# A selective scan: some input terms from a selected diagonal of B on TensorE, the skip term on TensorE, and one product with C for each pair of states

## The chip, the cores and the metric

The kernel runs on one core of a Trainium2 chip. The time is device time in microseconds (us) of one execution. Five engines work beside each other and meet only at semaphores: TensorE (PE in the profile; PEld is its weight load), VectorE (DVE), ScalarE (ACT), GpSimd (POOL) and SyncE (SP), which here issues all the DMAs. Each engine takes its instructions in program order.

## The reference

The whole program has four layers over an input of 4 images of 64 x 64 pixels with 96 channels: two convolution layers with a selective scan in four directions, and two layers of attention and feed-forward on tokens. The change lies in the selective scans of the first two layers. Cut to what matters, with K = 4 directions, 192 inner channels d and 16 states n:

```python
def _selective_scan(u, delta, A, Bs, Cs, Dp):
    ...
    def step(h, inp):
        u_l, dl, b_l, c_l = inp
        dA = jnp.exp(dl[..., None] * A)
        h = dA * h + (dl * u_l)[..., None] * b_l[:, :, None, :]
        y = jnp.einsum('bkdn,bkn->bkd', h, c_l)
        return (h, y)
    _, ys = lax.scan(step, h0, (u_t, d_t, B_t, C_t))
    ys = jnp.moveaxis(ys, 0, 3)
    return ys + Dp[None, :, :, None] * u
...
xs = jnp.concatenate([xs2, jnp.flip(xs2, axis=-1)], axis=1)
x_dbl = jnp.einsum('bkdl,kcd->bkcl', xs, x_proj_weight)
dts, Bmat, Cmat = jnp.split(x_dbl, [DT_RANK, DT_RANK + D_STATE], axis=2)
dts = jnp.einsum('bkrl,kdr->bkdl', dts, dt_projs_weight)
delta = jax.nn.softplus(dts + dt_projs_bias[None, :, :, None])
A = -jnp.exp(A_logs).reshape(K, D_INNER, D_STATE)
ys = _selective_scan(xs, delta, A, Bmat, Cmat, Dp)
```

So for each of 16 states, each channel holds a running value h over 4096 points: h = exp(delta A) h + (delta u) B. The output is the sum over the states of h C, plus the skip term D u.

## The kernel before, in words

Two images are worked on together (a pair), so there are four scans: two layers by two pairs. `PairScan.scan` does one. Its 192 channels by two images are laid out in three tiles of 128 partitions: tile j = 0 is image 0's first 128 channels, j = 1 is image 1's, and j = 2 holds the last 64 channels of both. A scan walks 4 directions k, in each 4 chunks ci of T = 1024 points, in each the three tiles j: 48 steps, named by `at`. Steps with j = 0 or 1 are called own here, those with j = 2 shared. A step has 16 states in 8 groups of NG = 2, named by `g`, with first state n0.

For each state a group needs three things of 128 x 1024. `da` is exp(delta A), made by ScalarE (`exp_of`, L522). `bp`, in PSUM, is delta u B; `cb` is C, read back by DMA from `crow` in DRAM and spread over the partitions. Who makes delta u B is written out by a letter for each state (L45, read by `maker`):

- V: TensorE spreads B over the partitions into bp by a product with the 0/1 table `sel` (two products of 512 columns); VectorE multiplies bp by `du` (L712).
- A: ScalarE makes the product with time on the partitions, where B is one scalar for a partition, in eight pieces `x` from `dut`, the transposed du (`outer`, L541); TensorE transposes the pieces back into bp.
- G: a DMA spreads B into `bb`, GpSimd multiplies it by du into `dbu` (`start_dbu`, L570), and bp then takes exp(delta A) instead.

VectorE runs the recurrence as one `tensor_tensor_scan` of 1024 points for each state (L715). GpSimd copies the last point to `last` for the next chunk (L728; not in the last chunk of a direction), then multiplies h by cb, one instruction for each state (L730). TensorE adds h up over the 16 states by transposing it into the PSUM tile `yp` (`add_up`, L603), with a lag of LAG = 3 groups; in direction 0 yp begins with the skip term, which ScalarE makes (`start_skip`, L631), and later with the sum of the directions before (`kept`). ScalarE copies yp out to `ysum` (`finish_sum`, L661). The projections for the next chunk and delta, du, dut of the next step are cut into pieces that are driven at fixed places between the groups (`project`, `discretise`, `drive`).

The program order is written out by hand. In group g's turn (loop at L680) come: the two bp of g; the sums of group g - 3; then, for g + 1, x and da (ScalarE), the loading of cb, and dbu (GpSimd); VectorE's products and the two scans of g; driven pieces; GpSimd's copy and products of g. What limits how far an engine runs ahead: bp has 2 buffers, da 4, x 2, h 4, cb 3, yp 1, dbu and bb 1. The wrapper `InOrder` (L56 to L73) keeps this order, and it is why all these instructions bear line L71 in the profile.

Of the kernel before, what the change touches and what calls it, by code (L numbers as in the profile page):

```python
# [16 lines left out]
F32 = mybir.dt.float32  # L17
BF16 = mybir.dt.bfloat16
# [8 lines left out]
HW = 64  # L27
# [14 lines left out]
LAG = 3  # L42


OWN, SHARED = "VAVAVAAGVAVAVAVA", "VGVAVAVGVAVGVAVV"  # L45
NT = L // 128
HID = 4 * C
EPS = 1e-5
# [36 lines left out]
class ScanLayer:  # L85


    def __init__(self, tc, pw, dram, x_src, w, n):
# [12 lines left out]

        self.amat = pw.tile([128, 2, K * NS], F32, name=f"amat{n}")
        nc.scalar.activation(self.amat, par[:, :, P_A : P_A + K * NS], AF.Exp)
        nc.vector.tensor_scalar(self.amat, self.amat, -1.0, None, ALU.mult)
        self.dsum = pw.tile([128, 2, 1], F32, name=f"dsum{n}")
        nc.vector.tensor_reduce(self.dsum, par[:, :, P_D : P_D + K], mybir.AxisListType.X, ALU.add)


class GroupNorm:
# [260 lines left out]
class PairScan:  # L370
# [5 lines left out]
    def __init__(self, tc, pk, pq, pd, cst, ident, u, layer, pr):  # L376
        self.tc, self.pk, self.pq, self.pd = tc, pk, pq, pd
        self.cst, self.ident, self.u = cst, ident, u
        self.par, self.amat, self.dsum = layer.par, layer.amat, layer.dsum
# [106 lines left out]

    def scan(self, stage, nc):
        tc, ident, steps, projected, made = self.tc, self.ident, self.steps, self.projected, self.made
        amat, dsum, w, y, weights, chunk_of = self.amat, self.dsum, self.w, self.y, self.weights, self.chunk_of
# [26 lines left out]
        of = (0, 128, 64)  # L516

        def maker(g, i):
            at, n0 = groups[g]
            return (SHARED if steps[at][2] == 2 else OWN)[n0 + i]  # L520
# [37 lines left out]
            return cb  # L558

        bbs = {}  # L560

        def start_bb(g):

            at, n0 = groups[g]
            for i in range(NG):
                if maker(g, i) == "G":
                    bbs[g, i] = p2.tile([128, 1, T], F32, name="bb", bufs=1)
                    spread(bbs[g, i], projected[at // 3][2], steps[at][2], 2 * NS + n0 + i)

        def start_dbu(g):  # L570
            out = {}
            for i in range(NG):
                if (g, i) in bbs:
                    out[i] = p2.tile([128, T], F32, name="dbu", bufs=1)
                    nc.gpsimd.tensor_tensor(out[i], made[groups[g][0]][1], bbs.pop((g, i))[:, 0], ALU.mult)
            return out

        def start_bp(g, i, xs):


            at, n0 = groups[g]
            _, _, j = steps[at]
            bp = pm.tile([128, T], F32, name="bp", bufs=2)
            if maker(g, i) == "G":
                exp_of(bp, g, i)
            elif maker(g, i) == "A":
                for t in range(T // 128):
                    nc.tensor.transpose(bp[:, 128 * t : 128 * t + 128], xs[i][:, t], ident)
            else:
                for hf in range(2):  # L590
                    cols = slice(512 * hf, 512 * hf + 512)
                    nc.tensor.matmul(
                        bp[:, cols],
                        sel[:, n0 + i, of[j] : of[j] + 128],
                        projected[at // 3][1][:, cols],
                        start=True,
                        stop=True,
                    )
            return bp
# [3 lines left out]
        def add_up(g, i, h):  # L603

            at, n0 = groups[g]
            n = n0 + i
            if n == 0:
                sums[at] = yp = pm.tile([128, T // 128, 128], F32, name="yp")
                if at in skips:
                    onto_time(yp, skips.pop(at), True, False)  # L610
                else:
                    before = kept.pop(at)
                    for t in range(0, T // 128, 4):
                        nc.tensor.matmul(yp[:, t : t + 4], ident, before[:, t : t + 4], start=True, stop=False)
            onto_time(sums[at], h[:, i], False, n == NS - 1)

        def onto_time(yp, v, first, final):

            for t in range(T // 128):
                nc.tensor.matmul(  # L620
                    yp[:, t],
                    v[:, 128 * t : 128 * t + 128],
                    ident,
                    start=first and t % 4 == 0,
                    stop=final and t % 4 == 3,
                    is_transpose=True,
                )

        skips = {}

        def start_skip(at):  # L631

            k, _, j = steps[at]
            if k == 0:
                skips[at] = p2.tile([128, T], F32, name="skip", bufs=1)
                nc.scalar.mul(
                    skips[at].rearrange("p (a b) -> p a b", b=HW), projected[at // 3][0][j], dsum[:, j // 2]
                )

        def places(at, tile_):  # L640
# [25 lines left out]

        for g in range(2):
            start_bb(g)
        ahead, cb_next, dbu_next = start_ahead(0), start_cb(0), start_dbu(0)
        hs = {}  # L670

        def sum_of(g):
# [7 lines left out]
        for g, (at, n0) in enumerate(groups):  # L680
# [12 lines left out]
            (da, xs), cb, dbu = ahead, cb_next, dbu_next  # L693
            if g + 2 < len(groups):
                start_bb(g + 2)

            bps = [start_bp(g, i, xs) for i in range(NG)]
            if g >= LAG:
                sum_of(g - LAG)
            if n0 == 0:  # L700
                start_skip(at)
            if n0 == NS - NG:
                drive(discretising, n0)
                drive(projecting, (j, n0))
            if g + 1 < len(groups):
                ahead, cb_next, dbu_next = start_ahead(g + 1), start_cb(g + 1), start_dbu(g + 1)

            hs[g] = h = p2.tile([128, NG, T], F32, name="h", bufs=LAG + 1)
            du = made[at][1]
# [16 lines left out]
            drive(projecting, (j, n0))  # L726
            if not final:
                nc.gpsimd.tensor_copy(last[j][:, n0 : n0 + NG], h[:, :, 0] if rev else h[:, :, T - 1])  # L728
            for i in range(NG):
                nc.gpsimd.tensor_tensor(h[:, i], h[:, i], cb[:, i], ALU.mult)  # L730
        for g in range(len(groups) - LAG, len(groups)):
            sum_of(g)
        finish_sum(len(steps) - 1)
# [206 lines left out]
def hybrid_kernel(ctx: ExitStack, tc: tile.TileContext, a):  # L940
# [14 lines left out]
    with ExitStack() as scans:  # L955
        pw = scans.enter_context(tc.tile_pool(name="s_w", bufs=1))
        pn = scans.enter_context(tc.tile_pool(name="s_n", bufs=1))
        units = []
        for n in range(2):
            layer = ScanLayer(tc, pw, dram, x, {k: a[f"l{n}_{k}"] for k in ("par", "wi", "wx", "wdt", "wo")}, n)  # L960
            units += [(layer, pr) for pr in range(NB // 2)]
            x = layer.x_dst
        units[0][0].after = units[2][0]
        with ExitStack() as scanning:
            pk = scanning.enter_context(tc.tile_pool(name="s_k", bufs=2))
            pu = scanning.enter_context(tc.tile_pool(name="s_u", bufs=1))
            pq = scanning.enter_context(tc.tile_pool(name="s_q", bufs=1))
            pd = scanning.enter_context(tc.tile_pool(name="s_d", bufs=2, space=DRAM))
            cst["sel"] = pu.tile([NP, NS, 256], BF16, name="sel")
            nc.sync.dma_start(out=cst["sel"], in_=a["c_sel"])  # L970
            cst["ident16"] = pu.tile([128, 128], BF16, name="ident16")
            nc.vector.tensor_copy(cst["ident16"], ident)
            u = [pu.tile([128, L], F32, name=f"u{j}") for j in range(3)]
            before = None
            for unit in units:
                scan = PairScan(tc, pk, pq, pd, cst, ident, u, *unit)
                between_scans(tc, cst, ident, half, pn, u, before, scan, unit)
                scan.run()
                before = unit
        token_layers(tc, cst, ident, half, x, before, a)  # L980


def constants():
# [10 lines left out]
    group = np.where(at[:, None] // 3 == at[None] // 3, np.float32(1) / np.float32(3), np.float32(0))  # L994
    heads = np.where(at[:, None] // 16 == at[None] // 16, np.float32(0.25), np.float32(0))
    return {
        "c_sel": sel.reshape(NP, NS, 256),
        "c_group": group.astype(np.float32),
        "c_heads": heads.astype(np.float32),
    }  # L1000
# [93 lines left out]
```

## Time and profile before

| What | Value |
|---|---|
| Time, median of 3 runs | 10596.84 us (10596.55 to 10597.79) |
| Profiled execution, first to last instruction | 10592.1 us |
| Instructions | 142441 |
| Mean granted TensorE clock | 0.885 of full |
| HBM traffic | 199 GB/s over the span |

How to read the lines below: in a group, the shape after the names is the output's and then the input's, `x` gives the count, after the first bar stand the time in which the group was busy (us) and the mean length of one instruction (ns), and after the second bar the engine's idle time just before these instructions, with what ended it. In a view in order of time, the columns are start (us), length (us), engine, line, operation, tiles, shape and count, and in brackets idle time with what ended it. In the list of waits: who waited for whom, then us in total, how often, and the longest. In a view by windows: the stretch, its length, then for each engine busy us and count of instructions.

### The profile page before, as it was taken

The page shows a single profiled execution, that of the slowest core. Times are in us where ns is not written, and L with a number is a line of the kernel's source. Part 1 is how long each engine was busy: PE and PEld are TensorE (multiplying, and loading weights), DVE is VectorE, ACT ScalarE, POOL GpSimd, SP SyncE. Part 2 cuts the span into 40 slices and gives each one's busy share as a digit, 9 for nine tenths or more (in the row PEclk, how much of TensorE's full clock was granted, in tenths as well). Part 3 has the DMA queues.
Part 4 walks back from the last instruction along what each step waited for, and adds up shares of the span by engine and source line. Part 5 has one row for each costly group of instructions (what it writes and reads, how often), then busy time and mean ns, then how long its engine had stood idle before and what let it go on. Part 6 is the DMA issues. An engine that isn't in the chain of part 4 may idle for free. (4 is left out here: it accounts for less than half of the span.)

```text
span 10592.1 us, 142441 instructions
## 1 busy us (share of the span) xinstructions
PE 8027.2 (76%) x47648; PEld 5946.6 (56%) x47648; DVE 9610.8 (91%) x6922; ACT 8761.4 (83%) x18779; POOL 9023.9 (85%) x5298
## 2 busy tenths in 40 slices
PE   7777777777777777777877777777877777777666
PEld 4555555554555555555555555555555565555554
DVE  8999999998999999998899999999799999999755
ACT  6888888885988888887788888888688888888666
POOL 3999999993999999997599999999399999999645
PEclk9888898989888898998888988898888989899877
DMA  5677777776677777777567777777667777777710
GB/s 155 208 212 216 220 220 218 219 218 164 205 212 212 218 220 218 217 220 210 158 206 213 219 220 220 223 213 216 162 207 212 216 213 225 221 217 213 195 32 25
DMA packets 905174, 2120.41 MB, mean 200 GB/s; under 512 B 330582, under 2 KB 640152, under 8 KB 706712
## 3 DMA queue, kind: packets, MB, share of 16 engines
q1 hardware_dynamic: 904440, 2111.30, 69.5%
q8 instruction: 378, 6.19, 0.3%
q14 instruction: 356, 2.92, 0.1%
HBM read 1949.56 MB, written 161.48 MB: 199 GB/s over the span
## 5 line engine op out<-in xcount | busy, mean ns | idle before, releaser
L71 POOL TENSOR_TENSOR h<-h,cb 128x1024 f32<-128x1024 f32 x3072 | 7196.5, 2367 | 226.4 <-issue 62.6
L71 DVE TENSOR_TENSOR_SCAN h<-da,last,bp 128x1024 f32<-128x1024 f32 x2064 | 4736.6, 2335 | 146.7 <-PE bp L71 22.8
L71 ACT ACTIVATE x<-dut,bt 128x128 f32<-128x128 f32 x12288 | 3495.9, 371 | 1.4 <-PE bp L71 1.1
L71 PE MATMUL yp<-ident,h 128*128 128x128 f32 x24576 | 3359.4, 297 | 10.5 <-POOL h L71 10.5
L71 PEld LDWEIGHTS yp<-ident,h 128*128 128x128 f32 x24576 | 3188.5, 157 | 126.6 <-issue 76.6
L71 ACT ACTIVATE da<-delta,amat 128x1024 f32<-128x1024 f32 x2752 | 3062.3, 1139 | 96.6 <-DVE h L71 95.8
L71 PE MATMUL bp<-ident,x 128*128 128x128 f32 x10240 | 1678.5, 316 | 1294.1 <-DVE h L71 956.8
L71 PEld LDWEIGHTS bp<-ident,x 128*128 128x128 f32 x10240 | 1361.3, 163 | 1854.8 <-ACT x L71 1017.4
L71 DVE TENSOR_TENSOR bp<-du,bp 128x1024 f32<-128x1024 f32 x1472 | 1780.5, 1214 | 259.8 <-PE bp L71 257.8
L71 DVE TENSOR_TENSOR_SCAN h<-da,bp 128x1024 f32<-128x1024 f32 x688 | 1537.7, 2275 | 49.9 <-ACT da L71 9.6
L71 PE MATMUL bp<-bparts,sel 96*128 96x512 bf16 x2944 | 920.5, 398 | 756.3 <-DVE h L71 740.4
L71 PEld LDWEIGHTS <-sel 96*128 96x128 bf16 x2944 | 226.8, 100 | 1550.2 <-DVE h L71 1037.8
L71 ACT ACTIVATE bp<-delta,amat 128x1024 f32<-128x1024 f32 x320 | 358.1, 1119 | 526.3 <-DVE h L71 524.6
L71 POOL TENSOR_TENSOR dbu<-du,bb 128x1024 f32<-128x1024 f32 x320 | 755.7, 2362 | 0.0
L71 DVE TENSOR_TENSOR_SCAN h<-bp,last,dbu 128x1024 f32<-128x1024 f32 x240 | 558.9, 2329 | 16.9 <-POOL dbu L71 15.9
L71 PE MATMUL xps<-u,wx 128*76 128x512 f32 x720 | 532.2, 824 | 0.0
L71 POOL COPY last<-h 128x2 f32<-128x2 f32 x1152 | 217.7, 189 | 357.2 <-DVE h L71 355.5
L81 POOL TENSOR_TENSOR ln_rs<-ln_ve,half 128x4 f32<-128x4 f32 x64 | 89.8, 1403 | 483.1 <-DVE ln_ve L79 405.9
L71 ACT ACT_TABLE_LOAD x380 | 487.5, 1283 | 15.9 <-PE bp L71 9.2
L71 POOL TENSOR_TENSOR du<-delta,u 128x1024 f32<-128x1024 f32 x188 | 496.8, 2642 | 0.0
L71 PE MATMUL dps<-cdt,wdt 12*128 12x512 f32 x752 | 433.6, 656 | 0.0
L71 ACT COPY ysum<-yp 128x1024 f32<-128x1024 f32 x192 | 194.5, 1013 | 287.1 <-PE yp L71 287.1
(159 smaller groups left out, 6312.6 us busy)
## 6 DMA issues: line engine op xcount, KB each, us to landing
cb<-crow SPq DMA_DIRECT2D x1024, 1024.0 KB
cb<-crow SPq DMA_DIRECT2D x1024, 512.0 KB
bb<-crow SPq DMA_DIRECT2D x384, 256.0 KB
bb<-crow SPq DMA_DIRECT2D x128, 512.0 KB
y<-ysum SPq DMA_DIRECT2D x192, 256.0 KB
kept<-y SPq DMA_DIRECT2D x160, 256.0 KB
y<-ysum SPq DMA_DIRECT2D x64, 512.0 KB
zt<-zg SPq DMA_DIRECT2D x64, 384.0 KB
```

The costliest lines, as they stand in the source:

```text
L71: return self.tc.keep_in_program_order(getattr(self.engine, op)(*args, **kwargs))
L81: nc.gpsimd.tensor_tensor(rs, ve, half, ALU.pow)
```

## The change

Three things change. In own steps three states of 16 get a new letter D, in place of V or A, the G goes, and the A move, so that the pairs read VD AA VD AA VD AA VA VA instead of VA VA VA AG VA VA VA VA. For a D, GpSimd's `affine_select` builds from the column of B (`bt`, time on the partitions) eight diagonal matrices of 128 x 128, and TensorE multiplies `dut` by them into bp; nobody else touches that bp before the scan. The selects of group g + 1 stand on GpSimd behind dbu of g + 1 and ahead of the copy and product of g. Second, the skip term is added by TensorE as a product of u with a diagonal of D that is made once a layer; ScalarE's instruction goes. Third, the product with C is one GpSimd instruction of 128 x 2048 for a group. Besides, the table sel is half as wide, and for own steps one column of it is spread as the weight.

```diff
@@ -42,7 +42,7 @@
-OWN, SHARED = "VAVAVAAGVAVAVAVA", "VGVAVAVGVAVGVAVV"
+OWN, SHARED = "VDAAVDAAVDAAVAVA", "VGVAVAVGVAVGVAVV"
...
@@ -104,6 +104,9 @@
         nc.vector.tensor_reduce(self.dsum, par[:, :, P_D : P_D + K], mybir.AxisListType.X, ALU.add)
+        self.skip = pw.tile([128, 2, 128], F32, name=f"skip{n}")
+        for s in range(2):
+            nc.vector.tensor_scalar(self.skip[:, s], ident, self.dsum[:, s], None, ALU.mult)
...
@@ -558,6 +559,7 @@
+        zero = self.tc.nc.gpsimd.to_reg(0.0)
...
+        def start_diagonals(g):
+
+            at, n0 = groups[g]
+            j = steps[at][2]
+            out = {}
+            for i in range(NG):
+                if maker(g, i) == "D":
+                    out[i] = p2.tile([128, T // 128, 128], F32, name="dg", bufs=1)
+                    col = NS * j + n0 + i
+                    nc.gpsimd.affine_select(
+                        out=out[i],
+                        in_=projected[at // 3][4][:, :, col : col + 1].to_broadcast([128, T // 128, 128]),
+                        compare_op=ALU.is_equal,
+                        fill=zero,
+                        base=0,
+                        pattern=[[0, T // 128], [-1, 128]],
+                        channel_multiplier=1,
+                    )
+            return out
...
-        def start_bp(g, i, xs):
+        def start_bp(g, i, xs, dgs):
...
+            elif maker(g, i) == "D":
+                for t in range(T // 128):
+                    nc.tensor.matmul(
+                        bp[:, 128 * t : 128 * t + 128], made[at][2][:, t], dgs[i][:, t], start=True, stop=True
+                    )
             else:
+                if j == 2:
+                    chosen = sel[:, n0 + i]
+                else:
+                    chosen = sel[:, n0 + i, D1 * j : D1 * j + 1].to_broadcast([NP, 128])
...
-                        sel[:, n0 + i, of[j] : of[j] + 128],
+                        chosen,
...
                 sums[at] = yp = pm.tile([128, T // 128, 128], F32, name="yp")
-                if at in skips:
-                    onto_time(yp, skips.pop(at), True, False)
+                k, ci, j = steps[at]
+                if k == 0:
+                    for t in range(T // 128):
+                        there = T * ci + 128 * t
+                        nc.tensor.matmul(
+                            yp[:, t],
+                            self.u[j][:, there : there + 128],
+                            self.skip[:, j // 2],
+                            start=t % 4 == 0,
+                            stop=False,
+                        )
                 else:
...
-        def start_skip(at):
-
-            k, _, j = steps[at]
-            if k == 0:
-                skips[at] = p2.tile([128, T], F32, name="skip", bufs=1)
-                nc.scalar.mul(
-                    skips[at].rearrange("p (a b) -> p a b", b=HW), projected[at // 3][0][j], dsum[:, j // 2]
-                )
...
-            bps = [start_bp(g, i, xs) for i in range(NG)]
+            bps = [start_bp(g, i, xs, dgs) for i in range(NG)]
             if g >= LAG:
                 sum_of(g - LAG)
-            if n0 == 0:
-                start_skip(at)
...
                 ahead, cb_next, dbu_next = start_ahead(g + 1), start_cb(g + 1), start_dbu(g + 1)
+                dgs_next = start_diagonals(g + 1)
...
                 nc.gpsimd.tensor_copy(last[j][:, n0 : n0 + NG], h[:, :, 0] if rev else h[:, :, T - 1])
-            for i in range(NG):
-                nc.gpsimd.tensor_tensor(h[:, i], h[:, i], cb[:, i], ALU.mult)
+            nc.gpsimd.tensor_tensor(h, h, cb, ALU.mult)
...
-            cst["sel"] = pu.tile([NP, NS, 256], BF16, name="sel")
+            cst["sel"] = pu.tile([NP, NS, 128], BF16, name="sel")
...
-    sel = np.zeros((3, 2, NS, NS, 2, 128), ml_dtypes.bfloat16)
+    sel = np.zeros((3, 2, NS, NS, 2, D1), ml_dtypes.bfloat16)
```

More of the change, by code (lines that the diff above doesn't have):

```diff
@@ L85, with __init__ @@
 class ScanLayer:
-    def __init__(self, tc, pw, dram, x_src, w, n):
+    def __init__(self, tc, pw, dram, ident, x_src, w, n):
         nc = tc.nc
@@ L378, in __init__ @@
         self.cst, self.ident, self.u = cst, ident, u
-        self.par, self.amat, self.dsum = layer.par, layer.amat, layer.dsum
+        self.par, self.amat, self.skip = layer.par, layer.amat, layer.skip
         self.w, self.y = layer.w, layer.y[pr]
@@ L488, in scan @@
         tc, ident, steps, projected, made = self.tc, self.ident, self.steps, self.projected, self.made
-        amat, dsum, w, y, weights, chunk_of = self.amat, self.dsum, self.w, self.y, self.weights, self.chunk_of
+        amat, w, y, weights, chunk_of = self.amat, self.w, self.y, self.weights, self.chunk_of
         sel = self.cst["sel"]
@@ L515, in scan @@
         groups = [(at, n) for at in range(len(steps)) for n in range(0, NS, NG)]
-        of = (0, 128, 64)
         def maker(g, i):
@@ L614, in add_up, with onto_time @@
                         nc.tensor.matmul(yp[:, t : t + 4], ident, before[:, t : t + 4], start=True, stop=False)
-            onto_time(sums[at], h[:, i], False, n == NS - 1)
-        def onto_time(yp, v, first, final):
+            onto_time(sums[at], h[:, i], n == NS - 1)
+        def onto_time(yp, v, final):
             for t in range(T // 128):
@@ L623, in onto_time @@
                     ident,
-                    start=first and t % 4 == 0,
+                    start=False,
                     stop=final and t % 4 == 3,
                     is_transpose=True,
-                )
-        skips = {}
-        def start_skip(at):
-            k, _, j = steps[at]
-            if k == 0:
-                skips[at] = p2.tile([128, T], F32, name="skip", bufs=1)
-                nc.scalar.mul(
-                    skips[at].rearrange("p (a b) -> p a b", b=HW), projected[at // 3][0][j], dsum[:, j // 2]
                 )
@@ L668, in scan @@
             start_bb(g)
-        ahead, cb_next, dbu_next = start_ahead(0), start_cb(0), start_dbu(0)
+        ahead, cb_next, dbu_next, dgs_next = start_ahead(0), start_cb(0), start_dbu(0), start_diagonals(0)
         hs = {}
@@ L692, in scan @@
                 load_kept(at + 1)
-            (da, xs), cb, dbu = ahead, cb_next, dbu_next
+            (da, xs), cb, dbu, dgs = ahead, cb_next, dbu_next, dgs_next
             if g + 2 < len(groups):
                 start_bb(g + 2)
-            bps = [start_bp(g, i, xs) for i in range(NG)]
+            bps = [start_bp(g, i, xs, dgs) for i in range(NG)]
             if g >= LAG:
                 sum_of(g - LAG)
-            if n0 == 0:
-                start_skip(at)
             if n0 == NS - NG:
@@ L959, in hybrid_kernel @@
         for n in range(2):
-            layer = ScanLayer(tc, pw, dram, x, {k: a[f"l{n}_{k}"] for k in ("par", "wi", "wx", "wdt", "wo")}, n)
+            layer = ScanLayer(tc, pw, dram, ident, x, {k: a[f"l{n}_{k}"] for k in ("par", "wi", "wx", "wdt", "wo")}, n)
             units += [(layer, pr) for pr in range(NB // 2)]
@@ L996, in constants @@
     return {
-        "c_sel": sel.reshape(NP, NS, 256),
+        "c_sel": sel.reshape(NP, NS, 128),
         "c_group": group.astype(np.float32),
```

## The prediction

> **What bounds the kernel now.** I read the page's busy times first, then the four scans alone (the view by windows), because their shares are averages over stages.
>
> ```profile
> PE 8027.2 (76%) x47648; PEld 5946.6 (56%) x47648; DVE 9610.8 (91%) x6922; ACT 8761.4 (83%) x18779; POOL 9023.9 (85%) x5298
> ...
> sum 9182.80, PE 6982.38 PEld 5296.28 DVE 8693.53 ACT 7948.40 POOL 8611.19; mean PE 1745.59 PEld 1324.07 DVE 2173.38 ACT 1987.10 POOL 2152.80
> ```
>
> The four scans take 9182.8 of 10592.1 us; all of the change but a few tiny instructions lies in them. There DVE is busy 94.7% and POOL 93.8%, ACT 87%. The chain of waits is no help: it accounts for some 5% of the span, all of it in the token layers at the end. So I worked by steps. A scan has 48, in triples j = 0, 1, 2; 9182.8 / 64 gives 143.5 us a triple. Next the costs, from the groups with shapes kept apart:
>
> ```profile
> L71 POOL TENSOR_TENSOR h<-h,cb 128x1024 f32<-128x1024 f32 x3072 | 7196.5, 2367 | 226.4 <-issue 62.6 <-PE dps L71 34.5 <-PE yp L71 20.0
> L71 DVE TENSOR_TENSOR_SCAN h<-da,last,bp 128x1024 f32<-128x1024 f32 x2064 | 4736.6, 2335 | 146.7 <-PE bp L71 22.8 <-DVE bp L71 2.8 <-ACT x L71 1.5
> L71 DVE TENSOR_TENSOR bp<-du,bp 128x1024 f32<-128x1024 f32 x1472 | 1780.5, 1214 | 259.8 <-PE bp L71 257.8
> L71 POOL TENSOR_TENSOR dbu<-du,bb 128x1024 f32<-128x1024 f32 x320 | 755.7, 2362 | 0.0
> L346 PE MATMUL po<-wo,gt 128*128 128x96 f32 x256 | 52.0, 287 | 0.0
> L345 PE MATMUL po<-wo,gt 128*128 128x96 f32 x256 | 51.9, 286 | 4.6 <-DVE gt L328 4.5
> ```
>
> Then one step on POOL and on DVE in order of time. Durations overlap a little, so I price by the distance from start to start:
>
> ```profile
> 885.41 0.19 POOL L71 COPY last<-h 128x2 f32<-128x2 f32 x1 [2.25 <-DVE h L71]
> 885.68 4.68 POOL L71 TENSOR_TENSOR h<-h,cb 128x1024 f32<-128x1024 f32 x2
> 890.31 2.36 POOL L71 TENSOR_TENSOR dbu<-du,bb 128x1024 f32<-128x1024 f32 x1
> 892.61 0.19 POOL L71 COPY last<-h 128x2 f32<-128x2 f32 x1
> ...
> 898.01 4.58 DVE L71 TENSOR_TENSOR_SCAN h<-da,last,bp 128x1024 f32<-128x1024 f32 x2
> 902.51 1.21 DVE L71 TENSOR_TENSOR bp<-du,bp 128x1024 f32<-128x1024 f32 x1
> 903.82 4.58 DVE L71 TENSOR_TENSOR_SCAN h<-da,last,bp 128x1024 f32<-128x1024 f32 x2
> ```
>
> POOL: 0.27 for the copy and 4.63 for two products, 4.90 a group; dbu 2.30. DVE: 2.25 a scan, 1.33 a product (1.31 here, 1.34 elsewhere in this step). Last, what each waits for:
>
> ```profile
> DVE bp L71 <- PE bp L71: 257.8, 325, 9.3
> ...
> DVE h L71 <- POOL dbu L71: 34.1, 27, 2.7
> ...
> POOL last L71 <- DVE h L71: 355.5, 242, 31.6
> ```
>
> DVE mostly waits for nothing, a little for TensorE; POOL's idle time is mostly waiting for DVE. DVE is the bound, POOL close behind.
>
> Ledger of a triple. DVE: an own step (j = 0, 1) 16 x 2.25 + 7 x 1.33 = 45.3, a shared one (j = 2, nine V) 48.0; triple 138.6, idle 4.9. POOL: an own step 8 x 4.90, du 2.6 (2.3 to 2.9 in this timeline), dbu 2.3, less 0.5 because the last chunk of four has no copies: 43.6; a shared one with three dbu and 0.6 for parts 48.8; triple 136.0, idle 7.5.
>
> **What the Trainium skill says.** "GPSIMD Engine Reference", section 3.1, gives a POOL fp32 tensor_tensor over 2048 elements 4497 ns; the trace has 2367 for 1024, so merging two saves at most 0.24 us; no run yet shows 2048. The same page, section 7, says that compare-and-select bodies can reach 1.03 cycles an element, and that reads of over 8 bytes' stride cost half as much again. The one select in this trace (making the identity, 128 x 128) took 294 ns and fits the first. "SBUF — State Buffer", section "Who interferes with whom", says that a DVE instruction with one SBUF input does not contend with GpSimd. The trace agrees: scans beside a busy POOL take 2335 on bp and 2329 with dbu. "TensorE: Matmul & The Clock Gate", Part 2, says that matmuls stay in program order, so a late bp holds the sums behind it; the trace's idle times before bp agree.
>
> ```profile
> 1.14 0.29 POOL masks.py:199 TENSOR_SCALAR_AFFINE_SELECT ident<-ident 128x128 f32<-128x128 f32 x1
> ```
>
> **The change part by part**, for each own step (32 a scan, 128 in all); a shared step keeps its letters.
>
> DVE loses two products, 2 x 1.33 = 2.7: own step 42.6, shared 48.0, triple 133.3.
>
> POOL loses a dbu, 2.3, and its bb transfer (512 KB of SP's traffic; DMA is 75% busy in the scans, so I give that nothing). It gains three selects of 1024 elements. The nearest row: 0.29 us for 128 elements, 0.19 for a two-element copy, so about 0.1 us for 126 elements. Eight blocks of that plus 0.19 is 1.0 us. Bounds: 0.9 from the page's 1.03 cycles; 2.35 if each of the eight blocks costs the 0.29 anew. I take 1.0, because the read has a zero inner step and no block needs its own instruction. The merged product saves between 0 and 0.24 us a group; I take 0.14, 1.1 a step. It now waits for both scans, but the copy ahead of it did so already, except in the last chunk. POOL's own step: 43.6 - 2.3 + 3.0 - 1.1 = 43.2; shared 47.7; triple 134.1.
>
> TensorE: a D is eight fp32 products of 128 columns. A true product and a transposing one cost the same (L345 and L346: 286 and 287 ns), and sixteen transposes for yp start within 1.75 us at the full clock, so D costs 0.9, like an A. Seven V (0.45), eight A, one G become five V, eight A, three D: +1.8 us on about 38 busy. It sits in the 2.2 us of the neighbour's scan; in the worst group TensorE has V, D and the sum, 0.45 + 0.9 + 1.75 = 3.1 against DVE's 5.8. At half clock this doubles and shows. The broadcast sel as weight changes two loads of 98 ns a V; even twice that hides there. The skip on TensorE replaces eight transposes by eight products (48 steps) and takes 1.1 us off ACT there; ACT has idle time, so nothing. The two diagonals at the start are four small DVE products: nothing.
>
> ACT: eight A before and after, one exp goes to SBUF instead of PSUM. That exp blocked ACT while bp was occupied (ACT bp on DVE h, 524.6 us over all 320 G); 128 of these go. But A now stands in pairs: two x of 2.34 and two exps of 1.04, 6.8 us in one group, and 2.1 in the next. Over two groups 8.9 against DVE's 10.3; da has four buffers, so a pair is covered.
>
> New wait: select, then D's products, then the second scan of that group. Queued behind it on TensorE are the sums and the next bp; on DVE the scan, and all later ones. POOL does the select after the products of group g-1 and before the copy of g: about 4.9 + 1.0 after the scan of g-1 ends, products 0.9, so 6.8. DVE gets there after 4.5 (an A,A group) + 1.33 + 2.25 = 8.1. Slack 1.3 us while POOL is not behind; POOL may be behind, and then DVE stands.
>
> The sum: with DVE's old idle time the triple is 133.3 + 4.9 = 138.2; with POOL as the bound and its old idle time 134.1 + 7.5 = 141.6. The two engines are now within 1 us, and tied by D, so I take the middle, 139.9. That is -3.6 x 64 = -230 us: span 10362. Runs lie 4.7 us above the profiled span (10596.84 against 10592.1), so 10367. The part's own bounds give -339 (10258) and -122 (10475).
>
> **Rivals.** (1) The select is dear, and POOL becomes the bound: slower. At 2.35 us POOL needs 134.1 + 6 x 1.35 = 142.2; with 4.9 idle, 147.1 a triple, +230: 10827. It decides from a select of 1.75 us: then POOL's triple is 138.6, what DVE's is now. For it: 384 new instructions on an engine 94% busy, and POOL's non-product rows cost more an element (the 128 x 128 products for the diagonals 607 ns). Against: the 294 ns. (2) The A,A bursts with softplus, its table loads and ysum in the same stretch (4.9 us of ACT at the third group) hold ACT, then yp, then bp. Such waits exist: DVE stands 0.94 at that place now. Two more us an own step give 143.9 a triple: 10622; half of that 10494. (3) POOL never holds DVE, all of DVE's saving is kept: 10258.
>
> **How the numbers follow.** Middle case 0.45; (3) at or below its number 0.05; the dear select 0.25; the bursts 0.17, of which 0.08 still faster, 0.04 equal, 0.05 slower; others slower (a slow clock exposing TensorE's added 1.8 us) 0.07; others equal 0.01. A difference of 0.2%, about 21 us, is what a measurement of this kernel can tell. Faster 0.58, same 0.05, slower 0.37. The likeliest case has 10260 to 10475 as its own range; to leave out no more than 2 in 10 the whole range reaches to 10800, into the dear select.
>
> **What would show it.** Right: the select at 1.0 to 1.2 us, the product over 2048 at 4.5, D's products at 0.11 apart, DVE products down to 1216, DVE's idle time in the scans about as now, POOL waiting less for DVE. Wrong: a select over 1.75; scans waiting for TensorE's bp behind POOL's dg; ysum late, seen as yp waiting for ACT; more idle time on DVE than it saved in products (343 us).

## The result: 0.6% slower, and the profile after

| | before | after |
|---|---|---|
| Time, median | 10596.69 us | 10652.82 us (10648.67 to 10656.37, 4 runs) |
| Ratio, 95% interval | | 1.0056 [1.0044, 1.0068] |
| Profiled span | 10592.1 us | 10646.9 us |
| Mean granted TensorE clock | 0.885 | 0.901 |

The forecast was 10367 us, faster; the change is slower. The busy times of the page after:

```profile
PE 8516.0 (80%) x53664; PEld 6576.3 (62%) x53664; DVE 9338.9 (88%) x6670; ACT 8738.0 (82%) x18731; POOL 8926.6 (84%) x4018
```

And the view by windows over the four scans of after:

```profile
sum 9226.90, PE 7463.32 PEld 5919.06 DVE 8416.13 ACT 7926.12 POOL 8503.13; mean PE 1865.83 PEld 1479.76 DVE 2104.03 ACT 1981.53 POOL 2125.78
```

Set against the same lines of before: in the scans DVE is busy 277.4 us less (8693.5 to 8416.1; the forecast had 343, counted from start to start), and POOL 108 less. Yet the scans last 44.1 us longer (9182.8 to 9226.9), so the time in which DVE is not busy grew by 321.5 us, from 489.3 to 810.8. The other 10.7 us of the span's growth lie between the scans. The question is where DVE stands. The groups of after, shapes apart:

```profile
L71 POOL TENSOR_TENSOR h<-h,cb 128x2048 f32<-128x2048 f32 x1536 | 6981.3, 4548 | 319.3 <-DVE h L71 168.1 <-issue 53.3 <-PE bp L71 3.0
L71 DVE TENSOR_TENSOR_SCAN h<-da,last,bp 128x1024 f32<-128x1024 f32 x2160 | 4957.4, 2335 | 395.4 <-PE bp L71 293.6 <-ACT da L71 2.1 <-POOL last L71 0.6
L71 PE MATMUL bp<-ident,x 128*128 128x128 f32 x10240 | 1477.8, 296 | 488.0 <-DVE h L71 437.1 <-ACT x L71 22.8 <-ACT ysum L71 19.4
L71 DVE TENSOR_TENSOR bp<-du,bp 128x1024 f32<-128x1024 f32 x1216 | 1473.1, 1216 | 276.0 <-PE bp L71 267.8
...
L71 PE MATMUL bp<-dg,dut 128*128 128x128 f32 x6144 | 972.5, 323 | 415.5 <-DVE h L71 210.2 <-POOL dg L71 199.4 <-DVE bp L71 5.8
...
L71 POOL TENSOR_SCALAR_AFFINE_SELECT dg<-bt 128x1024 f32<-128x1024 f32 x384 | 419.7, 1093 | 23.0 <-PE cps L192 21.9 <-DVE gn_norm L141 1.2
```

The select takes 1.09 us and the merged product 4.55: both as forecast. The scans' idle time behind bp went from 22.8 to 293.6 us. One count is not as forecast: 384 D, each of eight products, should be 3072 instructions, but `bp<-dg,dut` has 6144. The transposes of an A, 1280 A of eight pieces, do have the 10240 that one expects. **In these traces a true fp32 product stands as two instructions, a transpose as one.** The list of waits of after:

```profile
PEld bp L71 <- POOL dg L71: 507.6, 316, 2.7
...
DVE h L71 <- PE bp L71: 400.3, 341, 2.7
...
POOL last L71 <- DVE h L71: 365.9, 391, 7.4
...
DVE bp L71 <- PE bp L71: 267.8, 348, 9.3
...
PE bp L71 <- POOL dg L71: 199.4, 188, 2.2
```

Of the four signs against the forecast that it named, one is here in both its parts: scans that wait for bp, and TensorE waiting for `dg`. A second is met by the busy time: DVE's idle time grew by 321.5 us and its work fell by 277.4. The other two did not show: the select is not over 1.75 us, and yp waits less for ScalarE's `ysum` than before (68.8 to 36.4 us on TensorE, 106.1 to 67.1 on its weight load). POOL does not wait less for DVE (355.5 to 365.9). One place where DVE stands, the second group of an own step, in order of time, TensorE first, then DVE, then POOL:

```profile
917.21 0.60 PE L71 MATMUL bp<-bparts,sel 96*128 96x512 bf16 x2 [1.00 <-DVE h L71]
919.53 3.54 PE L71 MATMUL bp<-dg,dut 128*128 128x128 f32 x16 [1.72 <-DVE h L71]
922.86 2.08 PE L71 MATMUL yp<-ident,h 128*128 128x128 f32 x16
924.87 1.12 PE L71 MATMUL dps<-cdt,wdt 12*128 12x512 f32 x2
925.92 1.97 PE L71 MATMUL bp<-ident,x 128*128 128x128 f32 x16
...
919.30 1.21 DVE L71 TENSOR_TENSOR bp<-du,bp 128x1024 f32<-128x1024 f32 x1
920.64 2.35 DVE L71 TENSOR_TENSOR_SCAN h<-da,last,bp 128x1024 f32<-128x1024 f32 x1
923.17 2.35 DVE L71 TENSOR_TENSOR_SCAN h<-da,last,bp 128x1024 f32<-128x1024 f32 x1 [0.18 <-PE bp L71]
927.15 4.58 DVE L71 TENSOR_TENSOR_SCAN h<-da,last,bp 128x1024 f32<-128x1024 f32 x2 [1.62 <-PE bp L71]
...
918.13 1.09 POOL L71 TENSOR_SCALAR_AFFINE_SELECT dg<-bt 128x1024 f32<-128x1024 f32 x1
```

The same stretch by windows; the third number from the end is the granted TensorE clock:

```profile
917.20:919.50 2.30, 0.60 (x2) 0.11 (x2) 2.30 (x2) 2.30 (x6) 2.07 (x3) 1.00 0.27 53
919.53:922.86 3.33, 3.33 (x16) 3.33 (x17) 3.19 (x2) 2.90 (x8) 3.25 (x2) 0.54 0.93 356
```

D's bp comes free when the scan before ends, at 919.4, and the diagonal is there at 919.2. From then TensorE has to finish D, the sums, a piece of delta and the first A of the next group before DVE's next scan; the eighth of the sixteen transposes starts at 926.7. DVE needs 1.21 and twice 2.35 in that time and stands 1.62 us. The sixteen instructions of D stand 0.213 us apart here, half the rate of the transposes behind them (0.109, from 923.3 on): the granted clock, 1.00 until TensorE's wait ended, was 0.54 over D. This is not so for every D: 126 of the 384 ran mostly at the half clock.

### The profile page after: what moved, and what is told of

It reads as the page before. It is cut to its first block, busy times and chain, and to the rows that moved or that the text cites. A ratio compares the mean times of both kernels' runs of the same rounds, so it can differ in the third digit from the quotient of the medians.

```text
span 10646.9 us, 152820 instructions
## 1 busy us (share of the span) xinstructions
PE 8516.0 (80%) x53664; PEld 6576.3 (62%) x53664; DVE 9338.9 (88%) x6670; ACT 8738.0 (82%) x18731; POOL 8926.6 (84%) x4018
## 5 line engine op out<-in xcount | busy, mean ns | idle before, releaser
L71 POOL TENSOR_TENSOR h<-h,cb 128x2048 f32<-128x2048 f32 x1536 | 6981.3, 4548 | 319.3 <-DVE h L71 168.1
L71 DVE TENSOR_TENSOR_SCAN h<-da,last,bp 128x1024 f32<-128x1024 f32 x2160 | 4957.4, 2335 | 395.4 <-PE bp L71 293.6
L71 ACT ACTIVATE da<-delta,amat 128x1024 f32<-128x1024 f32 x2880 | 3207.1, 1140 | 285.6 <-DVE h L71 281.7
L71 PE MATMUL bp<-ident,x 128*128 128x128 f32 x10240 | 1477.8, 296 | 488.0 <-DVE h L71 437.1
L71 DVE TENSOR_TENSOR bp<-du,bp 128x1024 f32<-128x1024 f32 x1216 | 1473.1, 1216 | 276.0 <-PE bp L71 267.8
L71 PE MATMUL bp<-bparts,sel 96*128 96x512 bf16 x2432 | 751.6, 395 | 715.5 <-DVE h L71 598.6
L71 PE MATMUL bp<-dg,dut 128*128 128x128 f32 x6144 | 972.5, 323 | 415.5 <-DVE h L71 210.2
L71 PEld LDWEIGHTS bp<-dg,dut 128*128 128x128 f32 x6144 | 893.7, 231 | 606.2 <-POOL dg L71 507.6
L71 POOL COPY last<-h 128x2 f32<-128x2 f32 x1152 | 215.6, 187 | 405.3 <-DVE h L71 365.9
L71 POOL TENSOR_TENSOR dbu<-du,bb 128x1024 f32<-128x1024 f32 x192 | 452.8, 2359 | 0.0
L71 POOL TENSOR_SCALAR_AFFINE_SELECT dg<-bt 128x1024 f32<-128x1024 f32 x384 | 419.7, 1093 | 23.0 <-PE cps L192 21.9
```

The costliest lines, as they stand in the source:

```text
L71: return self.tc.keep_in_program_order(getattr(self.engine, op)(*args, **kwargs))
```

## The experiments

Ratios are to the kernel before on the same chip, with 95% intervals. "us" differences between two changed kernels are differences of their medians. Runs are grouped by question, not by order; some expectations refer to runs made earlier. A step's stalls by group are counted from the traces: DVE's waits of over 0.15 us, averaged over the 128 own steps.

### Which part of the change costs?

**letters_old**: the changed kernel with the letters of before; merged product, skip term on TensorE and narrow table stay.

```diff
-OWN = "VDAAVDAAVDAAVAVA"
+OWN = "VAVAVAAGVAVAVAVA"
```

> The letters of own steps as before (no D, no select); the merged product with C, the skip term on TensorE and the half-wide sel stay. TensorE theory: DVE is the bound again at its old work, the merged product only gives POOL slack: 10560 to 10600. If the merged product (which cannot start before both scans) or the new skip term is what costs: 10640 or more.

Measured 10600.55, 1.0002 [0.9994, 1.0011]. These three parts are worth nothing in this order of work, though POOL's busy time falls from 9024 to 8812 us: DVE is the bound. The whole loss is the letters'.

**d_short**: of a D's eight products seven become transposes of dut, nine instructions in place of sixteen; select and wait stay.

```diff
-nc.tensor.matmul(
-    bp[:, 128 * t : 128 * t + 128], made[at][2][:, t], dgs[i][:, t], start=True, stop=True
-)
+to = bp[:, 128 * t : 128 * t + 128]
+if t == 0:
+    nc.tensor.matmul(to, made[at][2][:, t], dgs[i][:, t], start=True, stop=True)
+else:
+    nc.tensor.transpose(to, made[at][2][:, t], ident)
```

> Of a D's eight blocks only the first is the product with the selected diagonal; blocks 1 to 7 are transposes of dut, so B is left out of the D states there. The select and the wait for it stay. TensorE theory (a true fp32 product is issued as two matmul instructions, so D is 16 of them, 1.79 us, and everything behind it is late): D falls to 9 instructions, about 1.0 us, DVE's waits for bp in own steps shrink by about half, time 10400 to 10530. Select theory (DVE is tied to POOL's select): time stays within 15 us of 10653.

Measured 10541.96, 0.9946 [0.9929, 0.9963]: 111 us below after. Without most of D's instructions the change is a gain, though a quarter of the forecast's, and less than expected: DVE's waits for bp fall from 668 to 581 us, not to half. At the place shown above DVE even stands 2.34 us instead of 1.62. D is short there, but the sums behind it run at the half clock (0.50 from 918 to 922):

```profile
916.14 0.77 PE L71 MATMUL bp<-dg,dut 128*128 128x128 f32 x2 [1.72 <-POOL dg L71]
916.70 1.70 PE L71 MATMUL bp<-ident,dut 128*128 128x128 f32 x7
918.19 3.62 PE L71 MATMUL yp<-ident,h 128*128 128x128 f32 x16
...
924.17 2.35 DVE L71 TENSOR_TENSOR_SCAN h<-da,last,bp 128x1024 f32<-128x1024 f32 x1 [2.34 <-PE bp L71]
```

So D's size is not what holds DVE at this place. It matters in the sixth group, where the stall falls from 0.86 to 0.23 us a step.

**select_once**: one diagonal is selected in a scan and used by every D.

```diff
+once = []
...
+if once:
+    out[i] = once[0]
+    continue
...
+once.append(out[i])
```

> The diagonal is selected once for a scan and read by every D, so 380 of 384 selects go and with them the wait for them; the B used in the D states is that of the first one. TensorE's work is unchanged. TensorE theory: POOL loses 400 us of work, but DVE still waits for bp behind TensorE: 10590 to 10645. Select theory: DVE's new idle time goes, 10350 to 10450.

Measured 10515.73, 0.9921 [0.9906, 0.9935]: 137 us below after. That lies between the two expectations. The edit takes away POOL's work and the wait together.

**short_and_once**: both edits.

> Both cuts at once: seven of a D's eight blocks are transposes of dut (9 instructions instead of 16, B left out there), and the diagonal is selected once for a scan (the first B is used in all D states). If the two costs are separate, they add: about 110 + 137 us off the changed kernel, 10390 to 10430. If they are one chain (POOL then TensorE then the scan, either cut enough), the time stays near the better of the two, 10490 to 10520. What is left over 10367 is then neither D's products nor the select.

Measured 10526.74, 0.9931 [0.9916, 0.9946], 126 below after: not more than select_once alone. The two costs are not a sum: each cut alone nearly ends the stall of the sixth group (0.86 us a step; 0.23 in d_short, 0.11 in select_once), and together they leave 1.36 of the second group's 1.74.

### Is it the select's work, its wait, or the pairs of A?

**early_select2**: the select is issued one group earlier, with two buffers; POOL does all its work.

```diff
-out[i] = p2.tile([128, T // 128, 128], F32, name="dg", bufs=1)
+out[i] = p2.tile([128, T // 128, 128], F32, name="dg", bufs=2)
...
-dgs_next = start_diagonals(g + 1)
+if g + 2 < len(groups):
+    dgs_of[g + 2] = start_diagonals(g + 2)
```

> The changed kernel with each select issued one group earlier (two ahead of its use, dg with two buffers). POOL does all its selects and products, only the wait of TensorE for dg goes. If the select costs by that wait: near select_once (10516), 10500 to 10550. If it costs by the 400 us of work on POOL: 10620 to 10655.

Measured 10542.23, 0.995 [0.9935, 0.9965]: 111 of select_once's 137 us. So most of the select's cost is when it comes, not POOL's time. In this run TensorE's wait for the diagonal is gone (4.1 us against 199.4), but what remains waits for DVE's bp:

```profile
L71 PE MATMUL bp<-dg,dut 128*128 128x128 f32 x6144 | 923.1, 313 | 281.0 <-DVE h L71 263.3 <-POOL h L71 13.6 <-POOL dg L71 4.1
```

**spread_letters**: no pairs of A in a group; D stands with an A and is the first of its group.

```diff
-OWN = "VDAAVDAAVDAAVAVA"
+OWN = "VADAVADAVADAVAVA"
```

> The changed kernel with the same letters (five V, three D, eight A) in another order: own steps are VA DA VA DA VA DA VA VA instead of VD AA VD AA VD AA VA VA. Each group has one A, so ScalarE's work is even, and a D is the first of its group, so TensorE makes it while the scan of the group ahead still runs. Selects, products and instruction counts are the same. If pairs of A and the place of D are what gives DVE's saving back: 10330 to 10480. If D's doubled products and the select cost it wherever they stand: 10600 to 10660.

Measured 11228.86, 1.0598 [1.0582, 1.0613], much slower: a miss. Its waits:

```profile
DVE h L71 <- PE bp L71: 916.6, 332, 4.3
PE bp L71 <- POOL dg L71: 652.8, 308, 3.9
```

As the first state of a group D is wanted one scan sooner than as the second, and the select stands at the same place on POOL. That is the wait's price when the slack is used up; of the pairs the run says nothing.

**spread_early_select2**: the same letters with the early select.

> spread_letters (11229) with the earlier selects. In spread_letters TensorE waits 900 us for dg, since a D that stands first in its group is wanted sooner than POOL's queue gives it. If that wait is the whole of its loss: the even ScalarE load shows, 10330 to 10480. If D's place costs by itself: 10700 or more.

Measured 10505.9, 0.9917 [0.9903, 0.9932]. The 5.98% loss was the wait: it is gone. Against early_select2 the spread letters are worth 36 us, less than expected. They move D to the front of its group as well, so this is not the price of the pairs alone.

**bursts_no_d**: the changed kernel without D, its places filled with V and one G, so that only the pairs remain. It has the same count of letters as letters_old.

```diff
-OWN = "VDAAVDAAVDAAVAVA"
+OWN = "VVAAVVAAVGAAVAVA"
```

> Own steps with the letters of the kernel before (seven V, eight A, one G), but with A in pairs as in the changed kernel: VV AA VV AA VG AA VA VA. No D and no select; the merged product and the new skip stay, as in letters_old (10600). If pairs of A alone cost: 10640 to 10750. If the loss needs D: 10585 to 10615.

Measured 10893.49, 1.0287 [1.0271, 1.0302]: more than expected, 293 us above letters_old for the order of letters alone. But it pairs V as well as A, so DVE's load is uneven too, and it is not the price of the pairs in the changed kernel. Its waits show the place, the V of a group behind the pair (2.3 us a step in the fifth group):

```profile
DVE bp L71 <- PE bp L71: 658.7, 521, 9.3
```

### Is it TensorE's order?

If the stretch between a freed bp and the next bp is too long, the sums should leave it. **sums_between** puts the sums of g - 3 between the two bp of g.

```diff
-bps = [start_bp(g, i, xs, dgs) for i in range(NG)]
+bps = [start_bp(g, 0, xs, dgs)]
 if g >= LAG:
     sum_of(g - LAG)
+bps.append(start_bp(g, 1, xs, dgs))
```

> The changed kernel with one move on TensorE: the sums of group g - 3 stand between the first and the second bp of group g, where TensorE waits for the scan anyway, instead of behind both. Nothing is left out. TensorE theory: the next group's first bp is no longer behind D and the sums, DVE's waits for bp shrink by more than half, 10350 to 10480. Select theory: no change, 10640 to 10660.

Measured 10753.1, 1.0145 [1.013, 1.016]: a miss. DVE's stall in the second group of own steps is gone, but the fourth group takes 10.3 us. There a new yp is opened, which waits until ScalarE has copied the old one; now the second bp stands behind that wait:

```profile
DVE h L71 <- PE bp L71: 479.1, 175, 5.3
PEld yp L71 <- ACT ysum L71: 422.2, 184, 2.6
PE yp L71 <- ACT ysum L71: 360.4, 183, 2.4
```

**sums_between_but_first** leaves the old order in the fourth group, in own and shared steps.

```diff
-if g >= LAG:
+if g >= LAG and n0 != NG * LAG:
     sum_of(g - LAG)
 bps.append(start_bp(g, 1, xs, dgs))
+if g >= LAG and n0 == NG * LAG:
+    sum_of(g - LAG)
```

> The changed kernel with the sums between the two bp, except in the fourth group of a step, where they open a new yp and so wait for ScalarE's copy of the old one; there they stay behind both bp. Nothing is left out. Order theory (D made a late bp later because TensorE's sums stood between it and the next bp): the waits of the second, fifth and sixth group go, 10100 to 10350. If the select alone held it: not below 10550.

Measured 10663.59, 1.0063 [1.0048, 1.0078], a miss. Against after, own steps improve (47.3 to 46.6 us each), shared ones get worse (49.8 to 51.5).

**before_sums_but_first**: the same order in the kernel before.

> The same move of the sums in the kernel before (letters, selects and products of the kernel before). DVE is 94.7% busy in its scans, so at most 490 us can go, and about 250 of those are waits for bp: 10350 to 10500 by the order theory. If DVE's waits for bp were due to something else: 10580 to 10610.

Measured 10539.52, 0.9937 [0.9921, 0.9954]. The old kernel gains from it, less than expected, with a smaller loss in shared steps (50.1 to 50.8).

**early_ysum**: as sums_between_but_first, and the copy of yp is issued earlier.

```diff
+if n0 == NG * (LAG - 1) and at > 0:
+    finish_sum(at - 1)
 bps.append(start_bp(g, 1, xs, dgs))
...
 drive(discretising, n0)
-if n0 == NG * (LAG - 1) and at > 0:
-    finish_sum(at - 1)
```

> As sums_between_but_first, and ScalarE's copy of yp is issued before the x and da of the next group instead of behind them and softplus, so that the new yp is free earlier. If the remaining wait of the fourth and fifth group is yp's: 20 to 100 us below sums_between_but_first. If ScalarE, now waiting at the copy for TensorE, delays x: equal or slower.

Measured 11024.66, 1.0403 [1.0387, 1.0418], a miss. ScalarE now stands at the head of its queue until the last sum is done, and everything behind the copy is late, dut first:

```profile
DVE bp L71 <- PE bp L71: 815.9, 322, 9.3
PEld dups L71 <- ACT dut L71: 737.2, 188, 5.8
...
ACT ysum L71 <- PE yp L71: 584.0, 128, 18.8
```

**before_own_sums**: the kernel before, new order in own steps alone.

```diff
-bps = [start_bp(g, i, xs) for i in range(NG)]
-if g >= LAG:
+between = g >= LAG and j < 2 and n0 != NG * LAG
+bps = [start_bp(g, 0, xs)]
+if between:
+    sum_of(g - LAG)
+bps.append(start_bp(g, 1, xs))
+if g >= LAG and not between:
     sum_of(g - LAG)
```

> The kernel before with the sums between the two bp in own steps alone (before_sums_but_first gained 0.7 us in an own step and lost 0.75 in a shared one): 128 x 0.7 = 90 us off, 10490 to 10530.

Measured 10461.18, 0.9876 [0.9861, 0.9891]: faster than both kernels of the case.

**spread_own_sums**: this order in the changed kernel with the spread letters and the late select.

> spread_letters, and in own steps the sums stand between the two bp (not in the fourth group, where they wait for ScalarE). TensorE then works while it waits for a scan. If its half-clock stretches and the queue behind bp still cost: 20 to 150 us below spread_letters. If only ScalarE is left: within 15 us of it.

Measured 11574.4, 1.0924 [1.0905, 1.0942], a miss: slower still than spread_letters. The wait for the diagonal decides again (TensorE 1068.5 us, its weight load 1362.9).

**early_own_sums2**: the changed letters, early select, sums between the bp in own steps.

> early_select, and in own steps the sums stand between the two bp, not in the fourth group (the move that took 133 us off the kernel before). If TensorE's queue is the second cost: 10400 to 10480. If pairs of A on ScalarE hold what is left: 10500 to 10560.

Measured 10467.55, 0.9881 [0.9864, 0.9897]: 75 us below early_select2, 185 below after. Its D and one stretch of its timeline:

```profile
L71 PE MATMUL bp<-dg,dut 128*128 128x128 f32 x6144 | 771.1, 280 | 18.2 <-DVE h L71 13.0 <-POOL dg L71 4.5
```

```profile
900.72 0.66 PE L71 MATMUL dups<-ident,du 128*128 128x128 f32 x4 [1.46 <-ACT dut L71]
901.22 1.87 PE L71 MATMUL xps<-u,wx 128*76 128x512 f32 x2
902.91 1.03 PE L71 MATMUL bp<-bparts,sel 96*128 96x512 bf16 x2
...
908.19 1.91 PE L71 MATMUL yp<-ident,h 128*128 128x128 f32 x16
910.10 2.02 PE L71 MATMUL bp<-dg,dut 128*128 128x128 f32 x16
...
903.98 1.23 DVE L71 TENSOR_TENSOR bp<-du,bp 128x1024 f32<-128x1024 f32 x1 [1.36 <-PE bp L71]
```

D follows the sums without a wait and runs at the full clock, 2.02 us in place of 3.54; of the 384 D 7 are now mostly at the half clock, not 126. The scans' wait for bp falls from 400.3 to 41.1 us, and the second group's stall from 1.52 in early_select2 to 0.01 a step. What is late now are the V at two places. One is this, in the eighth group, 1.17 us a step: TensorE stands for ScalarE's copies of the next step's dut, with V queued behind. The other is the fifth group, 1.21 a step: the fourth keeps the old order, and V stands behind both its A and its sums in the trace. No run takes this stall alone away.

**spread_early_sums2**: all three cuts.

> All three: letters spread, selects a group earlier, sums between the two bp in own steps. If wait, pairs of A and TensorE's queue were the three ways in which the saving went back, what was forecast is here or better: 10250 to 10400. If not, something that I have not named holds it.

Measured 10566.46, 0.9976 [0.9968, 0.9985], a miss: 99 us worse than without the spread.

```profile
L71 PE MATMUL bp<-dg,dut 128*128 128x128 f32 x6144 | 979.3, 326 | 375.5 <-DVE h L71 375.5
```

TensorE is busy 177 us longer than in early_own_sums2 (8584.0 against 8407.0) for the same instructions: as first of its group, D again stands after a wait for bp (375.5 us) and runs at the lower clock. Why it waits there was not taken apart further.

**early_sums_moved**: as early_own_sums2, with the pairs of A moved away from the copy of yp.

```diff
-OWN = "VDAAVDAAVDAAVAVA"
+OWN = "VDAAVDVDAAVAAAVA"
```

> As early_own_sums2, but the pairs of A stand in the second, fifth and seventh group (VD AA VD VD AA VA AA VA), so that none of them stands beside the copy of yp to ysum. Theory: the 1.2 us a step that VectorE still stands ahead of the fifth group come from a pair of A in the fourth group, where ScalarE also has ysum to make; then they fall below 0.4, and with the eighth group's 1.15 unchanged the time is 10350 to 10410. Rival: the pair at the seventh group meets the pieces of delta and du of the next step on ScalarE instead, the eighth group's stall grows over 2 us a step, and the time is 10470 to 10650.

Measured 10846.65, 1.024 [1.0223, 1.0257]. The fifth group, which now holds a pair of A, still waits for its bp, 1.6 us a step, so the copy of yp is not shown to be the cause. The eighth group's stall grew to 4.1 us a step, more than the rival said: the pair now meets the pieces of the next step on ScalarE, and dups waits for dut as in early_ysum:

```profile
DVE bp L71 <- PE bp L71: 624.6, 256, 9.3
PEld dups L71 <- ACT dut L71: 464.7, 128, 4.6
```

**letters_old_own_sums**: the changed kernel with the letters of before, sums between the bp in own steps.

> The changed kernel with the letters of before (so the merged product, the skip term on TensorE and the narrow table stay), and the sums between the two bp in own steps. Theory: these three parts are worth nothing here either, 10445 to 10480 as before_own_sums (10461). Rival one: with fewer waits on VectorE the merged product's shorter GpSimd time counts, 10400 to 10440. Rival two: the merged product gives h of the first state later to the sums, which now stand ahead of the second bp, and the time is 10490 to 10550.

Measured 10437.66, 0.9855 [0.9841, 0.987], the fastest of all. Its interval meets that of before_own_sums, so whether the merged product is worth something here isn't settled. Against early_own_sums2 the two sums by windows, over the scans of each (early_own_sums2 first):

```profile
sum 9046.00, PE 7361.06 PEld 5909.07 DVE 8414.50 ACT 7893.33 POOL 8489.25; mean PE 1840.27 PEld 1477.27 DVE 2103.63 ACT 1973.33 POOL 2122.31
```

```profile
sum 9020.10, PE 7009.08 PEld 5355.18 DVE 8684.57 ACT 7882.54 POOL 8384.00; mean PE 1752.27 PEld 1338.80 DVE 2171.14 ACT 1970.64 POOL 2096.00
```

With the letters of the change DVE has 270 us less to do and stands 296 us more (631.5 against 335.5). Even with its two main costs mended, the D letters bring nothing here.

## Why the prediction was wrong

The step that failed is the price and the cover of D on TensorE: "a D is eight fp32 products of 128 columns ... so D costs 0.9, like an A", and "3.1 against DVE's 5.8". With it went the slack given to the select, and the sum's term "DVE's old idle time": that idle time grew by 321.5 us. DVE's waits for bp in own steps alone grew from 174 to 539 us. By group they are, in us a step:

| Group | 1 | 2 | 3 | 4 | 5 | 6 | 7 | 8 |
|---|---|---|---|---|---|---|---|---|
| before | 0 | 0.73 | 0.05 | 0.19 | 0 | 0.02 | 0 | 0.38 |
| after | 0.32 | 1.74 | 0.13 | 0.07 | 0.64 | 0.86 | 0.28 | 0.17 |
| d_short | 0 | 1.61 | 0.01 | 0.13 | 1.05 | 0.23 | 0.47 | 0.15 |
| early_select2 | 0.24 | 1.52 | 0 | 0 | 0.72 | 0.11 | 0.48 | 0.36 |
| short_and_once | 0 | 1.36 | 0.01 | 0 | 1.28 | 0 | 0.69 | 0.21 |
| early_own_sums2 | 0.11 | 0.01 | 0 | 0 | 1.21 | 0.16 | 0.09 | 1.17 |

- **Size.** D is sixteen instructions 0.111 us apart at the full clock, 1.79 us and not 0.9. The comparison of L345 with L346 couldn't show it, as both are true products (the transposing row is L348). The counts could: L345 has 256 instructions for 128 calls in the code, L348 128 for 128. So could the Trainium skill, "FP8 and Floating Point Precision", section "TensorE Precision Notes", which gives true fp32 four passes; four times the 55.6 ns that "TensorE: Matmul & The Clock Gate", Part 1, gives for 128 warm columns is an estimate of 222 ns a product, and twice 0.111 agrees. What the size costs is the first and the sixth group: d_short takes away 111 us of the 286 by which the result lies above the forecast.
- **The wait for the select.** "Slack 1.3 us while POOL is not behind": TensorE's instructions of D waited 199.4 us for `dg`, their weight loads 507.6 (the two overlap). early_select2 shows 111 us for that. It ends the same stall of the sixth group, so the two can't be added: short_and_once, 126 us below after, won no more than select_once and is still 160 above the forecast.
- **Cover.** I compared V, D and the sums with a group of DVE. What must fit is what TensorE does from the freed bp to the next bp: D, sums, a piece of delta, half of the next pair. At full clock and true size that is 1.79 + 1.75 + 1.05 + 0.87 = 5.5 us against DVE's 1.34 + 2 x 2.35 = 6.0; it fits, barely. At the half clock it does not, with a short D either. "At half clock this doubles and shows" was written down and given 0.07. Ahead of the second group of after, 104 of 128 own steps had 2.9 us or more of half clock in this stretch, and DVE waited 2.03 us there on average, against 0.48 in the other 24, which had none; in d_short it is 1.86 in 111 steps and nothing in 17. The two go together in the traces; no run changes the clock alone, so the clock is not shown to be the cause. What is shown is the order: with the sums out of this stretch the second group's stall is gone (early_own_sums2).
- **What is left.** The fifth and the seventh group, where V comes behind a pair of A, make up 0.92 us of waits a step that the kernel before did not have. Neither cut at D helps there, and the cause is open.
- **In short,** a ledger of busy times for two engines within 1 us of each other has no term for an in-order queue between them.
- **Right:** the select (1.0 forecast, 1.09 measured; from it the dear select fell), the merged product (4.5, and 4.55), D's instructions 0.11 apart (but two for each product), DVE's products down to 1216, the skip term and the table at nothing, POOL's own saving (1.9 us a triple forecast; its busy time fell 108 / 64 = 1.7).
- **The rival of the bursts** came near in number, 10622, but its path, ScalarE, then yp, then bp, is not what the trace of after shows: yp waits less for `ysum` than before, and TensorE's bp less for ScalarE's `x` (312.0 to 137.8 us). The late yp shows in sums_between. That the pairs cost by another path, in the fifth and the seventh group, is not ruled out.

Open: what limits the changed kernel after select and order are mended. Stalls of V behind ScalarE's dut copies and behind the fourth group's sums are seen in the trace, but in the mended order both other arrangements of the A made a longer wait elsewhere. The same D with one instruction a product was not tried.

## What to carry to other kernels

Work that goes from a busy engine to one with free time must fit where it is put in that engine's queue: take the stretch from the buffer's release to the next hand-over and add up all that is queued in it, at the lower clock too. Count instructions against calls in the old trace before pricing a new matmul by a similar one. And try the order of the queue first: moving the sums between the two bp gained 1.2% in the old kernel, which the whole change did not.

## What the runs showed of the hardware

- An fp32 product of 128 columns is two instructions in the trace, 2 x 0.111 us at the full clock; an fp32 transpose of the same size one, 0.109 us.
- TensorE at half rate after short waits: after 1.00 and 1.72 us of idle time the instructions of D stood 0.213 us apart, at a granted clock of 0.54. "TensorE: Matmul & The Clock Gate", Part 1, speaks of an idle window of some 3.4 us; here TensorE was idle for 2.7 of the 3.3 us ahead of D, with a V between the two waits.
- affine_select with a zero inner step in its input: 1.09 us for 128 x 1024, where 128 x 128 took 0.29: about 0.11 us for each further 128 elements. GpSimd's product over 2048 elements took 4.55 us, two of 1024 4.68 together.
